# Where the adjacency's checks are computed: row sums and zero-or-one test in the convolutions' passes, casting transfers in the attention stage

## The chip, the core and the metric

The kernel runs on one core of one Trainium2 chip. The time is the device time of one execution in microseconds (us). A core has a matrix engine (TensorE, PE in the profile, with its weight loads as PEld), a vector engine (VectorE, DVE), an engine for activations (ScalarE, ACT), a general one (GpSimd, POOL) and SyncE (SP), which here only issues transfers. Each takes its instructions in a fixed order; they meet at semaphores. Transfers (DMA) are issued by SP, ACT or POOL and moved by 16 DMA engines.

## What is computed

Sixteen graphs (batches) of N = 1024 nodes with D = 128 features each and a symmetric zero-or-one adjacency go through four residual layers, each after a layer norm and a relu:

```python
h = relu(layernorm(x)); x = x + three_convolutions(h, dilate(adj))   # layer 0
h = relu(layernorm(x)); x = x + attention(h, adj)                    # 4 heads, log(adj) added to the scores
h = relu(layernorm(x)); x = x + graph_attention(h, adj)              # 4 heads, softmax over neighbours
h = relu(layernorm(x)); x = x + normalised_sum(h, adj)               # layer 3
...
A_hat = adj + eye; deg = sum(A_hat, axis=2); d_inv = deg ** -0.5     # used in layer 3
```

Layer 0 removes neighbours row by row, then convolves three times: `agg = adj_d @ h / deg`, `out = agg @ Wr + h @ Wx + b`, rows normalised, relu, and a batch norm over all nodes of all graphs, which forces one pass over all sixteen graphs per convolution.

## The kernel before

The program has three stages after a short one for the weights. `P` = 128 rows make a block, so a graph has `NB` = 8 blocks; `HN` = 512 is half a row.

`dilate_plain` (to about 690 us) holds all sixteen adjacencies in fp8, loaded by casting transfers that POOL issues (L727, L729: 32-bit in memory, fp8 in the core), and writes the thinned ones to memory as `kept`, with the reciprocal degrees `rdeg`.

`convolutions_plain` (about 690 to 1604 us) makes a first pass over the graphs (layer norm, transposes, the neighbours' sum), two middle passes (convolution l = 0 and 1 with the sum for the next one) and a last one. A scheduler orders its instructions. In `neighbours`, one graph's thinned adjacency `C` (1 MB) and its reciprocal degrees spread over the partitions, `rdb` (512 KB), come in by SP; `h` is transposed into `hT`, split into three bf16 parts on ACT and DVE (L676 to L679), and 48 matmuls (`g`, L1040) make the sum, which DVE scales into `aggT` (L1042). A convolution reads `aggT` and `hT` (`o`, L1093 and L1094), squares on ACT (`sq`, L1099), sums on DVE (L1100), takes a power on POOL (L1045) and applies it on ACT (`h`, L1106). `hT` goes to memory as `spill`.

`attentions_plain` (about 1604 us to the end) runs layers 1 to 3 of several graphs side by side. Seven generators (`matrices`, `before`, `attend`, `values`, `positive`, `gat`, `gcn`) each yield an engine, an expected duration, the time that they need and a change in the number of PSUM banks; the planner `in_order` picks the step that can start first and so writes out one order for all engines. `before` loads `x` and the three `spill`ed results (`h_a`, `hT_a`, by SP) and finishes layer 0. `attend` puts the adjacency into PSUM (L1408, ACT), adds the scores (L1413, PE) and takes the exponential (L1421, ACT). `positive` and `gat` are layer 2, `gcn` is layer 3.

`matrices` brings in the untouched adjacency of each graph in fp8, as `A` (four buffers), and computes what the program must know of it. For each of the eight row blocks it loads 512 KB in 32 bits (L1309, two buffers), and ACT turns it into fp8 and sums the rows at the same time into `deg` (L1310). DVE tests that each value is zero or one, with the count of others in `trouble` (L1314). PE subtracts the transposed blocks (L1321, L1323) and ACT sums the absolute difference (L1327), which tests the symmetry. At the end `verdict` looks at `trouble`, and a slow general version, which is not needed for these inputs, runs if anything was found.

Of the kernel before, what the change touches and what calls it, by code (L numbers as in the profile page):

```python
# [6 lines left out]
F32 = mybir.dt.float32  # L7
# [11 lines left out]
P = 128  # L19
# [942 lines left out]
def convolutions_plain(tc, x, ident, ap, xp, h0, minus_half, kept, rdeg, spill, final, Wr, Wx, bias, gamma, beta, Wl, bl):  # L962
    nc = tc.nc
    with ExitStack() as ctx:
# [3 lines left out]
        w2 = ctx.enter_context(tc.tile_pool(name="c_work", bufs=2))  # L968
        pso = ctx.enter_context(tc.tile_pool(name="c_out", bufs=4, space=PSUM))
# [50 lines left out]
        def neighbours(b, h):  # L1020

            C = ap.tile([P, NB, N], F8, name="C")
            nc.sync.dma_start(C, kept[b])
            rdb = w2.tile([P, N], F32, name="rdb")
            nc.sync.dma_start(rdb, rdeg[b][None, :].to_broadcast([P, N]))
            for hf in range(2):
                ps = pst.tile([P, HN], F32, name="t")
                for c in range(4):
                    nc.tensor.transpose(ps[:, c * P:(c + 1) * P], h[:, 4 * hf + c, :], ident)  # L1029
                nc.scalar.copy(hT[b][:, hf * HN:(hf + 1) * HN], ps)  # L1030
            parts = w2.tile([P, 3, NB, D], BF16, name="parts")
            for m in range(2):
                half = slice(4 * m, 4 * m + 4)
                Splitter(nc)(h[:, half], [parts[:, k, half] for k in range(3)])
            for hf in range(2):
                cols = slice(hf * HN, (hf + 1) * HN)
                ps = psg.tile([P, HN], F32, name="g")
                for j in range(NB):
                    for k in range(3):
                        nc.tensor.matmul(ps, parts[:, k, j, :], C[:, j, cols],  # L1040
                                         start=j == 0 and k == 0, stop=j == NB - 1 and k == 2)
                nc.vector.tensor_tensor(aggT[b][:, cols], ps, rdb[:, cols], op=ALU.mult)  # L1042

        def rsqrt(out, v):
            nc.gpsimd.tensor_tensor(out, v, minus_half[:, :v.shape[-1]], op=ALU.pow)  # L1045

        for b in range(B):
# [15 lines left out]
            neighbours(b, h)  # L1063
            if b == 1:
                wr = [matrix(w, f"wr{i}") for i, w in enumerate(Wr)]
                wx = [matrix(w, f"wx{i}") for i, w in enumerate(Wx)]
                wl = final[:3]
                for i, t in enumerate(wl):
                    nc.sync.dma_start(t, Wl[i * D:(i + 1) * D])
                gam = [column(v, f"gam{i}") for i, v in enumerate(gamma)]  # L1070
                bet = [column(v, f"bet{i}") for i, v in enumerate(beta)]
                b6 = [row6(v, f"b6_{i}") for i, v in enumerate(bias)]
                last = row6(bl, "bl6")

        wr_s, wx_s, constant = wr[0], wx[0], row_parts(b6[0], "const0")
        for l in range(3):
            stats = kp.tile([P, 2 * B, 6], F32, name="stats")
            for b in range(B):
                if l:
                    rd6 = xp.tile([6, N], F32, name="xt")  # L1080
                    nc.sync.dma_start(rd6, rdeg[b][None, :].to_broadcast([6, N]))
                    has = w2.tile([6, N], BF16, name="has")
                    nc.vector.tensor_scalar(has, rd6, floor, None, op0=ALU.is_gt)
# [19 lines left out]
                rsqrt(nrm[:, 1, :], nrm[:, 0, :])  # L1103
                h = w2.tile([P, NB, D], F32, name="h")
# [3 lines left out]
                if l < 2:  # L1108
                    neighbours(b, h)
                else:  # L1110
                    for hf in range(2):
# [23 lines left out]
            if l < 2:  # L1135
# [4 lines left out]
                row = small.tile([6, D], F32, name="row")  # L1140
# [8 lines left out]
        nc.vector.tensor_copy(final[3][0:3], row_parts(last, "const3")[0:3])  # L1149

# [55 lines left out]
def attentions_plain(tc, x, spill, final, ready_weights, adj, deg, trouble, eye, out, scores, bound, reach):  # L1206
    nc = tc.nc
    with ExitStack() as ctx:
# [7 lines left out]
        lp = ctx.enter_context(tc.tile_pool(name="f_load", bufs=2))  # L1216
# [28 lines left out]
        nc.vector.memset(trouble, 0.0)  # L1245
# [54 lines left out]
        def matrices():  # L1300

            for b in range(B):
# [3 lines left out]
                for i in range(NB):  # L1306
                    t = yield "ACT", 1.3, 0.0, 0
                    a = lp.tile([P, N], F32, name="a")
                    nc.sync.dma_start(a, adj[b, i * P:(i + 1) * P, :])  # L1309
                    nc.scalar.activation(m[:, i, :], a, AF.Relu, accum_out=deg[:, b, i:i + 1], saturate=False)  # L1310
                    yield "DVE", 1.4, 0.0, 0
                    junk = lp.tile([P, N], F8, name="junk", bufs=1)

                    nc.vector.scalar_tensor_tensor(junk, a, 0.0, a, op0=ALU.is_gt, op1=ALU.not_equal,  # L1314
                                                   accum_out=trouble[:, b, i, 0:1], saturate=False)
                    for hf in range(2):
                        w = min(HN, (i - 4 * hf) * P)
                        if w > 0:
# [8 lines left out]
                            nc.scalar.activation(junk[:, :w], ps[:, :w], AF.Abs, accum_out=trouble[:, b, i, 1 + hf:2 + hf])  # L1327
# [412 lines left out]
def whole(tc, x, adj, nodemask, chunk_mats, chunk_mask, eye, sel, p, out):  # L1740
    nc = tc.nc
    with tc.tile_pool(name="dram", bufs=1, space=DRAM) as dp, tc.tile_pool(name="keep", bufs=1) as kp:
# [7 lines left out]
        trouble = kp.tile([P, B, NB, 3], F32, name="trouble")  # L1750
# [11 lines left out]
        with tc.tile_pool(name="final", bufs=1) as fp:  # L1762
            final = [fp.tile([P, D], F32, name=f"final{i}") for i in range(3)] + [fp.tile([3, D], BF16, name="final_row")]
            with tc.tile_pool(name="early", bufs=1) as yp, tc.tile_pool(name="c_adj", bufs=2) as ap, \
                    tc.tile_pool(name="c_x", bufs=2) as xp:
                ident = yp.tile([P, P], F32, name="ident")
                nc.sync.dma_start(ident, eye)
                minus_half = yp.tile([P, NB], F32, name="minus_half")
# [4 lines left out]
                convolutions_plain(tc, x, ident, ap, xp, h0, minus_half, kept, rdeg, spill, final, *layer0)  # L1773
# [46 lines left out]
```

## Time and profile before

| What | us |
|---|---|
| Runs before (three) | 4033.46, 4037.02, 4050.93; median 4037.02 |
| The profiled execution | 4039.04, span 4037.3 |
| PE busy | 3474.4 (86%) |
| DVE busy | 2527.9 (63%) |
| ACT busy | 2401.7 (59%) |
| POOL busy | 794.7 (20%) |
| Mean granted TensorE clock | 0.926 |

The page divides the span into 40 slices of 101 us; each digit is the busy share of a slice in tenths. The rows for PE, DVE, ACT and DMA show the three stages: dilation in the first seven slices, convolutions in the next nine, attention after that.

```profile
PE   4888887999999987778989988998898989989775
DVE  4988774543344343328776876776777686777656
ACT  3778764543333334676667776767666767766540
DMA  9632223443333312411221221122122022111000
```

A line of a group names the source line, the engine, the operation, the tile written and those read, the shape and the number of instructions; then busy time, mean nanoseconds of one, the engine's idle time before them and what ended most of it. [...]

### The profile page before, as it was taken

Reading aid. Unit: us, or ns where it says so; the run is one execution under the profiler, and the core shown is the slowest. Engines: PE = TensorE matmul, PEld = TensorE weight load, DVE = VectorE, ACT = ScalarE, POOL = GpSimd, SP = SyncE. Lnnn points to the kernel's source line nnn. Section 1 sums busy time; section 2 is a strip of 40 time slices with the busy share of each in tenths; the row PEclk is TensorE's granted clock in tenths of the full one; section 3 lists DMA queues with packets and bytes.
Section 4 is the critical chain, followed back from the end, with each engine's and each line's share of the span. In section 5 each row is a group of like instructions: output and inputs, shape, how many; then the busy total and the mean of one; then the engine's idle time right before and its main releaser. Section 6 shows DMA issues by size and latency. Waiting matters only on the chain.

```text
span 4037.3 us, 65855 instructions
## 1 busy us (share of the span) xinstructions
PE 3474.4 (86%) x26756; PEld 1998.6 (50%) x26756; DVE 2527.9 (63%) x4782; ACT 2401.7 (59%) x3961; POOL 794.7 (20%) x680
## 2 busy tenths in 40 slices
PE   4888887999999987778989988998898989989775
PEld 2556565445555566324444444444454444454333
DVE  4988774543344343328776876776777686777656
ACT  3778764543333334676667776767666767766540
POOL 7545521210000011101111112112111101211110
PEclk9999887999999998799999998999998999999887
DMA  9632223443333312411221221122122022111000
GB/s 106 40 21 16 14 97 116 165 159 126 125 111 121 108 68 85 142 37 53 74 79 43 64 79 60 51 74 74 43 69 80 26 74 79 58 59 48 27 17 17
DMA packets 182500, 293.21 MB, mean 73 GB/s; under 512 B 77468, under 2 KB 124456, under 8 KB 173992
## 3 DMA queue, kind: packets, MB, share of 16 engines
q1 hardware_dynamic: 91944, 221.69, 16.8%
q0 software_dynamic: 79728, 24.66, 7.5%
q10 hardware_dynamic: 10512, 42.54, 2.6%
q8 instruction: 212, 3.47, 0.4%
q14 instruction: 104, 0.85, 0.1%
HBM read 287.98 MB, written 51.19 MB: 84 GB/s over the span
## 4 chain that ended last, share of the span: by engine, by line
PE 58%; DVE 15%; ACT 7%; DMA 3%; issue 2%; POOL 2%; ACTq 0%; SPq 0%; POOLq 0%; DVEq 0%
PE g L1040 12%; PE acc L1444 9%; PE sum L1570 9%; PE t L1413 5%; PE sum L1624 4%; PE sum L1555 4%; DVE pm L1495 3%; PE o L1093 2%; PE sum L1357 2%; PE o L1094 2%; PE sum L1375 1%; ACT e L1421 1%; DVE rden L1450 1%; PE t L1029 1%; PE sum L1295 1%
## 5 line engine op out<-in xcount | busy, mean ns | idle before, releaser
L1421 ACT ACTIVATE e<-t 128x1024 f32<-128x1024 f32 x512 | 508.2, 1023 | 489.3 <-PE t L1413 472.9
L1495 DVE SCALAR_TENSOR_TENSOR pm<-dst,minus,A 128x1024 fp8e4<-128x1024 f32 x512 | 676.2, 1350 | 7.9 <-DMA dst<-scores 7.9
L1040 PE MATMUL g<-C,parts 128*128 128x512 fp8e4 x2304 | 521.3, 381 | 15.4 <-DVE aggT L1042 9.2
L1408 ACT ACTIVATE t<-A 128x2048 f32<-128x2048 fp8e4 x256 | 482.3, 1884 | 3.9 <-ACT dst L1475 0.3
L1570 PEld LDWEIGHTS <-pm 128*128 128x128 fp8e4 x4096 | 347.0, 98 | 187.1 <-issue 165.3
L1570 PE MATMUL sum<-parts,pm 128*128 128x198 bf16 x4096 | 400.3, 251 | 26.0 <-DVE pm L1495 16.3
L1444 PE MATMUL acc<-e,va 128*32 128x512 f32 x2048 | 330.5, 616 | 41.3 <-ACT e L1421 38.4
L1040 PEld LDWEIGHTS <-parts 128*128 128x128 bf16 x2304 | 223.1, 98 | 262.7 <-ACT parts L678 5.7
L1413 PE MATMUL t<-qT,kT 32*128 32x512 f32 x2048 | 307.7, 672 | 31.7 <-ACT t L1408 31.3
L1444 PE MATMUL acc<-e,ones_hd 128*32 128x512 f32 x2048 | 319.7, 601 | 0.0
L1573 DVE TENSOR_REDUCE pos<-sum 128x132 f32<-128x396 f32 x256 | 145.0, 566 | 204.0 <-PE sum L1570 203.4
L1555 PE MATMUL sum<-parts,A 128*128 128x396 bf16 x1024 | 210.8, 351 | 44.2 <-DVE parts L1547 23.9
L1042 DVE TENSOR_TENSOR aggT<-g,rdb 128x512 f32<-128x512 f32 x96 | 66.2, 690 | 269.2 <-PE g L1040 269.1
L1045 POOL TENSOR_TENSOR nrm<-nrm,minus_half 128x8 f32<-128x8 f32 x48 | 79.6, 1662 | 639.8 <-DVE nrm L1102 639.8
L1624 PE MATMUL sum<-A,gparts 128*128 128x512 fp8e4 x768 | 178.0, 385 | 24.9 <-ACT gparts L1607 17.6
L835 DVE TENSOR_TENSOR r<-ya,both 128x512 bf16<-128x512 f16 x184 | 140.2, 776 | 92.7 <-ACT ya L832 91.9
L1099 ACT ACTIVATE sq<-o 128x512 f32<-128x512 f32 x96 | 55.8, 599 | 226.1 <-PE o L1094 224.3
L1267 POOL TENSOR_TENSOR ln_st<-ln_st,minus_half 128x8 f32<-128x8 f32 x48 | 86.1, 1794 | 511.8 <-DVE ln_st L1265 377.1
L882 DVE SCALAR_TENSOR_TENSOR rows<-y,thirty,rows 128x1024 fp8e4<-128x1024 f16 x128 | 169.9, 1335 | 25.4 <-ACT y L874 24.6
L1555 PEld LDWEIGHTS <-A 128*128 128x128 fp8e4 x1024 | 94.5, 99 | 182.0 <-issue 104.1
L1106 ACT ACTIVATE h<-o,nrm 128x128 f32<-128x128 f32 x384 | 105.7, 384 | 116.9 <-POOL nrm L1045 113.7
L885 POOL TENSOR_TENSOR own<-rows,lower 128x256 bf16<-128x256 fp8e4 x128 | 109.5, 866 | 330.6 <-DVE rows L882 197.2
(287 smaller groups left out, 6937.7 us busy)
## 6 DMA issues: line engine op xcount, KB each, us to landing
a<-in_adj_dram SPq DMA_DIRECT2D x128, 512.0 KB
C<-kept SPq DMA_DIRECT2D x48, 1024.0 KB
dst<-scores SPq DMA_DIRECT2D x64, 512.0 KB
rdb<-rdeg SPq DMA_DIRECT2D x48, 512.0 KB
spill<-hT ACTq DMA_DIRECT2D x48, 512.0 KB
kept<-rows ACTq DMA_DIRECT2D x16, 1024.0 KB
h_a<-spill SPq DMA_DIRECT2D x64, 256.0 KB
hT_a<-spill SPq DMA_DIRECT2D x16, 512.0 KB
```

The source lines that it names most:

```text
L835: nc.vector.tensor_tensor(r, ya, both[:, 1, :, None].to_broadcast([P, G, P]), op=ALU.is_equal)
L882: nc.vector.scalar_tensor_tensor(row, y16, hh[:, g:g + 1], row, op0=ALU.not_equal, op1=ALU.mult, saturate=False)
L1040: nc.tensor.matmul(ps, parts[:, k, j, :], C[:, j, cols], start=j == 0 and k == 0, stop=j == NB - 1 and k == 2)
L1408: nc.scalar.activation(s, A[b][:, k, None, cols].to_broadcast([P, H, HN]), AF.Copy, scale=16.0)
L1413: nc.tensor.matmul(s[:, hd], kT[r, k * P:(k + 1) * P], qT[r, cols], start=False, stop=True, skip_group_check=True)
L1421: nc.scalar.activation(es[:, hd:hd + 2], s[:, hd:hd + 2], AF.Exp, scale=SIGMA)
L1444: nc.tensor.matmul(ps[r], ones if one else va[:, k, r], es[:, hd], start=k == 0, stop=k == NB - 1)
L1495: nc.vector.scalar_tensor_tensor(pm[:, i, :], dst[hd], minus[:, i, hd:hd + 1], A[b][:, i, :], op0=ALU.is_ge, op1=ALU.mult, saturate=False)
L1555: nc.tensor.matmul(ps[:, :3 * H * W], A[b][:, i, j * P:(j + 1) * P], parts4[:, i, :, :, W:], start=i == 0, stop=i == NB - 1)
L1570: nc.tensor.matmul(ps[:, jj * 6 * W:(jj + 1) * 6 * W], pm[:, i, (j + jj) * P:(j + jj + 1) * P], flat(parts4[:, i, hd]), start=i == 0, stop ...
L1573: nc.vector.reduce_sum(pos[:, j:j + 2, hd, :], ps[:, :12 * W].rearrange("p (j s w) -> p j w s", j=2, s=3), axis=AX.X)
L1624: nc.tensor.matmul(ps, parts[:, k, m, :], A[b][:, m, cols], start=m == 0 and k == 0, stop=False)
```

## The change

The row sums and the zero-or-one test leave the attention stage. A new function `look(n)` in the convolutions does n half row blocks (128 x 512): it loads one (256 KB, SP, three buffers), sums its rows on ACT with a relu whose result is thrown away, and tests it on DVE. It is called at several points of each pass, 256 times in all, and the two half sums are added into `deg` at the end of the stage. In the attention stage `matrices` loads each row block straight into fp8 by a casting transfer that POOL issues; the symmetry test stays. For room in the core's memory `rdb`, `has`, `row` and the attention's load pool get one buffer instead of two or three. `trouble` gets four columns, and its clearing moves to the start of the program, to POOL.

```diff
+        lp = ctx.enter_context(tc.tile_pool(name="c_load", bufs=3))
...
-            rdb = w2.tile([P, N], F32, name="rdb")
+            rdb = w2.tile([P, N], F32, name="rdb", bufs=1)
...
                 nc.scalar.copy(hT[b][:, hf * HN:(hf + 1) * HN], ps)
+            look(1)
             parts = w2.tile([P, 3, NB, D], BF16, name="parts")
...
+        halves = cp.tile([P, B, NB, 2], F32, name="halves")
+        parts_of = [(b, i, hf) for b in range(B) for i in range(NB) for hf in range(2)]
+
+        def look(n):
+
+            for b, i, hf in [parts_of.pop(0) for _ in range(n)]:
+                cols = slice(hf * HN, (hf + 1) * HN)
+                a = lp.tile([P, HN], F32, name="a")
+                nc.sync.dma_start(a, adj[b, i * P:(i + 1) * P, cols])
+                m = lp.tile([P, HN], F8, name="m", bufs=1)
+                nc.scalar.activation(m, a, AF.Relu, accum_out=halves[:, b, i, hf:hf + 1], saturate=False)
+                junk = lp.tile([P, HN], F8, name="junk", bufs=1)
+                nc.vector.scalar_tensor_tensor(junk, a, 0.0, a, op0=ALU.is_gt, op1=ALU.not_equal,
+                                               accum_out=trouble[:, b, i, 2 + hf:3 + hf], saturate=False)
...
             neighbours(b, h)
+            look(3)
...
-                    has = w2.tile([6, N], BF16, name="has")
+                    has = w2.tile([6, N], BF16, name="has", bufs=1)
...
                 rsqrt(nrm[:, 1, :], nrm[:, 0, :])
+
+                look(2 if l < 2 else 1)
...
                 if l < 2:
                     neighbours(b, h)
+                    look(2)
                 else:
+                    look(1)
...
-                row = small.tile([6, D], F32, name="row")
+                row = small.tile([6, D], F32, name="row", bufs=1)
...
+        nc.vector.tensor_tensor(deg, halves[:, :, :, 0], halves[:, :, :, 1], op=ALU.add)
...
-        lp = ctx.enter_context(tc.tile_pool(name="f_load", bufs=2))
+        lp = ctx.enter_context(tc.tile_pool(name="f_load", bufs=1))
...
-        nc.vector.memset(trouble, 0.0)
...
                 for i in range(NB):
-                    t = yield "ACT", 1.3, 0.0, 0
-                    a = lp.tile([P, N], F32, name="a")
-                    nc.sync.dma_start(a, adj[b, i * P:(i + 1) * P, :])
-                    nc.scalar.activation(m[:, i, :], a, AF.Relu, accum_out=deg[:, b, i:i + 1], saturate=False)
-                    yield "DVE", 1.4, 0.0, 0
-                    junk = lp.tile([P, N], F8, name="junk", bufs=1)
-
-                    nc.vector.scalar_tensor_tensor(junk, a, 0.0, a, op0=ALU.is_gt, op1=ALU.not_equal,
-                                                   accum_out=trouble[:, b, i, 0:1], saturate=False)
+                    t = yield "POOL", 0.9, 0.0, 0
+                    nc.gpsimd.dma_start(m[:, i, :], adj[b, i * P:(i + 1) * P, :])
+                    t += 8.0
...
+                nc.gpsimd.memset(trouble, 0.0)
```

## The prediction

> **What bounds the kernel now.** I read the table of busy time by stretch first. The dilation ends at about 690 us, the convolutions at about 1604 us, the attention stage at the end. Columns: stretch, length, then busy microseconds of PE, PEld, DVE, ACT and POOL with counts, granted clock, DMA share, GB/s.
>
> ```profile
> 690.00:747.00 57.00, 44.22 (x198) 22.30 (x197) 32.21 (x140) 27.87 (x61) 14.54 (x11) 0.83 0.51 167
> 747.00:923.00 176.00, 174.57 (x891) 90.03 (x889) 83.99 (x232) 83.88 (x191) 26.64 (x20) 1.00 0.45 159
> 923.00:1460.00 537.00, 513.49 (x2831) 311.22 (x2830) 213.38 (x384) 193.59 (x478) 50.23 (x32) 0.97 0.32 116
> 1460.00:1604.00 144.00, 119.83 (x800) 97.37 (x799) 54.96 (x103) 69.91 (x192) 27.21 (x16) 0.87 0.15 58
> 1604.00:1850.00 246.00, 184.92 (x1114) 81.62 (x1118) 96.74 (x187) 171.69 (x250) 26.73 (x15) 0.87 0.30 95
> 1850.00:3500.00 1650.00, 1478.46 (x11155) 790.38 (x11148) 1182.39 (x1749) 1136.14 (x1548) 270.23 (x142) 0.95 0.20 63
> 3500.00:3750.00 250.00, 218.94 (x1691) 117.47 (x1689) 189.04 (x251) 155.87 (x203) 30.90 (x15) 0.97 0.17 52
> 3750.00:4037.00 287.00, 200.64 (x1364) 110.81 (x1364) 170.83 (x246) 101.74 (x128) 38.52 (x22) 0.82 0.07 21
> ```
>
> TensorE is the bound nearly everywhere: 99% busy in the first pass (747 to 923), 96% in the two middle passes, 90% in the steady attention stage. The change takes nothing from PE. So it can gain only where PE idles in the attention stage (61 + 172 + 31 + 86 = 350 us) and lose where it makes PE idle in the convolutions, where ACT and DVE are only 36 to 48% busy.
>
> Next the groups that move, and PE's waits from 1850 to 3500 us (engine and line, what it waited for, total us, times, longest).
>
> ```profile
> L1314 DVE SCALAR_TENSOR_TENSOR junk<-a 128x1024 fp8e4<-128x1024 f32 x128 | 157.9, 1233 | 23.8 <-DMA a<-in_adj_dram 23.5
> L1310 ACT ACTIVATE A<-a 128x1024 fp8e4<-128x1024 f32 x128 | 135.3, 1058 | 31.4 <-DMA a<-in_adj_dram 31.4
> ```
> ```profile
> PE sum L1295 <- DVE oT L1452: 27.8, 5, 9.1
> PE t L1413 <- ACT t L1408: 27.1, 16, 4.0
> PE sum L1357 <- DMA h_a<-spill: 22.6, 9, 6.1
> PE sum L1321 <- ACT A L1310: 13.6, 4, 6.2
> PE sum L1555 <- DVE tot L1558: 13.3, 11, 3.0
> PE sum L1555 <- DVE parts L1547: 12.1, 4, 4.5
> ```
>
> PE's idle time is many short waits with different releasers; only L1310 and part of h_a belong to the work that leaves.
>
> Last, the SP queue's own waits and two pairs of pieces from the chain, which give the passes' rhythm.
>
> ```profile
> SPq L1309 <- DVE junk L1314: 885.9, 116, 65.8
> ```
> ```profile
> 747.04 20.33 PE g L1040 x92
> 771.02 19.86 PE g L1040 x92
> ...
> 923.34 9.50 PE g L1040 x44
> ...
> 974.25 9.50 PE g L1040 x44
> ```
>
> The first says that the adjacency loads, with two buffers, hold SP's queue until DVE has read them, and the loads behind them (h_a, hT_a) with it. The others: two batches take 24 us in the first pass, three take 50.9 us in the middle ones.
>
> [...]
>
> **Part by part, attention stage.**
> Removed: on ACT 128 × (1.058 + 0.196 accumulator read, source view of L1310) = 160 us, on DVE 128 × (1.233 + 0.083) = 168 us, on SP 128 issues of 0.33 us and the queue's blocking. Added on POOL: 128 casting issues; L727, the same form, takes 0.59 us each, 76 us on an engine that is 16% busy. They stand in front of the `pow` steps on POOL, at most one or two issues at a time (the order of the built program shows mostly one to three), so 1 us on a few chains, taken as nothing. Landing: 9.8 us in the crowded start of the dilation, 4.4 to 4.9 for 64 to 80 KB later. The planner allows 8 us before PE's symmetry check; from 0 to about 30 us of PE waiting, I take 0. PE's checks L1321 to L1323 and ACT's L1327 stay.
>
> What PE gains:
> - Start (1604 to 1850): PE idles 61 us and ACT is 70% busy. The chain here has 5.4% on adjacency loads, 3.2% on L1310 and 4.7% on h_a loads, of 246 us: 13 + 8 + 12. The first two go, half of the third (its other half is that buffer's own release): 27, less 2 for the casting loads that start with the stage: 25 us. Bounds 10 to 40.
> - Steady stretch: A 13.6, half of h_a 11; waits ended by ACT or DVE otherwise sum to about 135 us in the same view. ACT falls from 69 to 62%, DVE from 72 to 65%. As an estimate a queueing wait goes with u/(1-u), so 27% of what is queueing; I take a third of 135 as that, the rest as plain latency: 12. Sum 36 us. Bounds 5 (latency is the whole of it) to 90.
> - From 3500 on: the chain is latency of the last batches; 0, from -10 to +15.
> Together 61 us.
>
> **Convolutions.** Added: 256 pieces (128x512 each). On ACT 0.60 (L1099, the same width) + 0.20 - 0.1 overlap, so 0.70 to 0.80, 0.75 taken: 192 us. On DVE 0.68 (L1100) + 0.08: 195 us. On SP 256 issues of 0.33 = 84 us and 67 MB. The scheduler pulls the pieces forward: in the built program ACT has 81 before the first spill, 125 during the first of the two middle passes, 50 in the second, none later. Per three batches that is 25 pieces.
> - Room in a middle pass: 50.9 us less 36% that ACT is busy = 32.5, over 25: 1.30 us a piece. In the first pass, nine per pair: (24 - 11.4)/9 = 1.40.
> - Need: with three buffers a buffer's round is issue 0.33 + landing 2.95 + operation 0.75 + hops 0.25 = 4.3, so 1.43 us a piece once the three loaded ahead are used, 0.75 before. ACT takes them in groups of 8, 2, 2, 6, 1, 1, 5: 15 are loaded ahead, 10 paced, mean 1.02. It fits, so PE's matmuls should hide most of it.
> - What isn't hidden: DVE and ACT steps on the path from o to g (sq, norm, pow, h, transposes, parts) come up to a piece later each; g already starts within 1 us of its parts. I take 0.5 us per batch over 27 batches with pieces = 14 us, bounds 0 and 40. At the start, batch 1's normalisation stands behind five pieces and the second rdb load behind eight: 5 × 1.43 = 7 us, plus 3.
> - rdb, has and row with one buffer: the next rdb load waits for the product of the batch before, but it is needed only about 10 us later, at the first half's end; nothing. C is issued about 11 us before use; six pieces in front cost 3 × 0.33 + 3 × 1.43 = 5 us and its landing about 5: just covered, and if not, the loss is part of the rival below.
> - The memset of trouble on POOL goes ahead of the dilation's first loads: 1 us.
> Together 25 us. DMA share in a middle pass: 116 + 25 × 0.262 MB / 50.9 us = 245 GB/s; 116 is a share of 0.32, so about 0.68.
>
> **Sum.** The profiled execution took 4039.0 us (span 4037.3). 4039 - 61 + 25 = 4003; it lies 2 us above the median of the runs shown, so 4001.
>
> **Rivals.**
> 1. Slower: the pieces pace the passes. In SP's one queue, C and rdb wait for a batch's end, and pieces behind them wait along; pieces that load beside a 1 MB C land in 4.7 us (the longest such wait on a 256 or 512 KB load in the chain) and not 2.95. Then a round is 6.0, 2.0 us a piece, none loaded ahead. Against the room of 1.30 and 1.40 that is 175 × 0.7 + 81 × 0.6 = 171 us at worst; I put it at a mean of 1.8: 175 × 0.5 + 81 × 0.4 = 120, less 61: 4096. It decides from a mean of about 1.57 us on, where the loss reaches the gain. For it: three buffers, engines in order, PE at 96 to 99% with nothing to spare. Against it: groups are short, ACT has half its time free.
> 2. Nothing: the attention stage's waits are latency, gain 30, loss 25: 4032.
> 3. More: the lighter ACT and DVE let the planner pack PE; all 36 becomes 90 and the start gives 40: 3930.
> That the casting loads come late (30 us of PE waits) would turn the main case into the second.
>
> **Numbers.** Forecast 0.47 (own range 3955 to 4017), rival 3 0.10, rival 2 0.15, rival 1 0.28. About 0.5%, 20 us, is what a measurement tells from no change: faster 0.57, same 0.15, slower 0.28. Range 3920 to 4095: the steady stretch's upper bound below; above, rival 1 up to its central price.
>
> **What will show it.** Right: L1310 and the full-row L1314 gone; attention from its first to last instruction about 60 us shorter with ACT near 62% in the middle; first exponential earlier; first and middle passes with PE still over 93% busy and rhythms under 25 and 53 us. Wrong: PE waiting for C or parts in the passes, ACT's pieces waiting for adjacency loads by more than 50 us in sum with `sq` or `h` behind them; or PE's L1321 waiting for the casting loads.

## The result, and the profile after

The changed kernel takes 4025.81 us (median of 20 runs), the kernel before 4041.07 us in the runs beside it: ratio 0.9969, interval 0.9959 to 0.9978. By the ratio that is a gain of 0.3%, about 13 us (the medians are 15 us apart), where 36 us were forecast. The profiled executions are only 3 us apart, with spans of 4037.3 us before and 4034.2 us now, and the parts below are read from these two.

The small difference hides two large ones. The batch norm's `scale` on POOL ends each convolution, so the last of its three starts marks the border between the convolutions and the attention stage. The view of that tile gives number, durations in nanoseconds, and first and last start, first for the kernel before, then for the changed one:

```profile
L1045 POOL TENSOR_TENSOR scale<-mv,minus_half x3: 552/552/552, 1153.3 to 1605.9; 128x1 f32<-128x1 f32 x3
```
```profile
L1047 POOL TENSOR_TENSOR scale<-mv,minus_half x3: 552/553/553, 1242.4 to 1714.4; 128x1 f32<-128x1 f32 x3
```

The convolutions are 109 us longer (25 forecast), and the attention stage is 2319.8 us instead of 2431.4, 112 us shorter (61 forecast). Of the 109 us, 89 are there before the first `scale`.

Busy time by stretch in the changed kernel; the borders are the three `scale` steps and two points in the attention stage (columns as in the prediction's first table):

```profile
690.00:950.00 260.00, 225.64 (x1062) 114.48 (x1059) 166.11 (x542) 165.37 (x413) 39.20 (x30) 0.92 0.69 230
950.00:1242.40 292.40, 245.02 (x1264) 148.25 (x1264) 172.59 (x401) 176.24 (x475) 26.11 (x15) 0.92 0.64 211
1242.40:1552.70 310.30, 282.35 (x1566) 171.38 (x1564) 149.56 (x312) 137.24 (x354) 27.13 (x18) 0.94 0.43 150
1552.70:1714.40 161.70, 136.02 (x850) 105.34 (x850) 62.06 (x121) 69.88 (x192) 27.73 (x18) 0.84 0.14 55
1714.40:1962.00 247.60, 202.60 (x1313) 93.50 (x1316) 81.99 (x153) 160.40 (x215) 37.82 (x39) 0.91 0.28 54
1962.00:3602.00 1640.00, 1514.77 (x11562) 806.24 (x11555) 1122.02 (x1607) 1076.88 (x1407) 318.34 (x239) 0.97 0.21 44
3602.00:4034.20 432.20, 340.45 (x2451) 190.14 (x2449) 282.44 (x413) 194.20 (x252) 69.39 (x43) 0.89 0.10 24
```

PE is 87 and 84% busy in the first two stretches, where the kernel before has 94% up to 923 us and 97% from there to its first `scale` (these lines stand in the last section), while ACT and DVE are no more than 59 to 64% busy. Not one engine is full: they wait for each other. What ACT and DVE wait for stands in the groups of the page (busy us, mean ns, idle before and its cause):

```profile
L1063 DVE SCALAR_TENSOR_TENSOR junk<-a 128x512 fp8e4<-128x512 f32 x256 | 176.0, 688 | 146.2 <-DMA a<-in_adj_dram 142.7
L1061 ACT ACTIVATE m<-a 128x512 fp8e4<-128x512 f32 x256 | 161.9, 632 | 171.7 <-DMA a<-in_adj_dram 168.6
```

Each piece costs about as much waiting as working. From the chain of waits of the stretch 890 to 950 us (start, length, what):

```profile
895.16 7.07 DMA a<-in_adj_dram
...
905.54 8.15 DMA a<-in_adj_dram
...
914.56 3.41 DMA a<-in_adj_dram
...
919.69 6.73 DMA rdb<-rdeg
...
932.41 8.32 DMA a<-in_adj_dram
...
941.58 2.53 DMA a<-in_adj_dram
```

SP issued `C` and `rdb` just ahead of the three long ones (`rdb` at 894.75, 905.12 and 931.99): a piece of 256 KB that is issued right behind them takes 7 to 8 us, and `rdb` itself 6.7. Two pieces that are issued 9 to 10 us after `rdb` take 3.4 and 2.5 us. What this does to PE is in PE's waits from 690 us to the first `scale`, of the kernel before and of the changed one (total us, times, longest):

```profile
PE g L1040 <- DVE aggT L1042: 9.2, 3, 4.1
PE t L1029 <- ACT h L1106: 7.5, 5, 1.5
```
```profile
PE g L1042 <- DVE aggT L1044: 33.8, 16, 4.6
PE t L1030 <- ACT h L1128: 25.3, 5, 7.1
PE g L1042 <- ACT parts L678: 10.9, 8, 3.1
PE g L1042 <- DVE parts L679: 7.1, 3, 4.1
```

PE hardly waits for a piece itself. It waits for the convolution's own steps, and those stand behind a piece in ACT's or DVE's queue, which waits for its load. Three middle graphs take 61 to 62 us instead of 50.9 (the powers on POOL start at 1011.68, 1072.61, 1134.81 and 1196.37): 25 pieces in 61.5 us are 2.46 us a piece, a round of 7.4 us for each of three buffers. SP waited 253 times for a reader to free a buffer (169 times for DVE, 84 for ACT, 417 us in all), about as often as there are loads, so the buffers do pace them.

One such stretch in the timeline of the changed kernel, of ACT and then of DVE (start, us; in brackets the wait and its cause):

```profile
1123.33 0.63 ACT L1061 ACTIVATE m<-a 128x512 fp8e4<-128x512 f32 x1 [7.00 <-DMA a<-in_adj_dram]
```
```profile
1123.34 0.69 DVE L1063 SCALAR_TENSOR_TENSOR junk<-a 128x512 fp8e4<-128x512 f32 x1 [4.77 <-DMA a<-in_adj_dram]
...
1126.78 0.69 DVE L1063 SCALAR_TENSOR_TENSOR junk<-a 128x512 fp8e4<-128x512 f32 x1 [0.80 <-DMA a<-in_adj_dram]
1127.93 0.69 DVE L1063 SCALAR_TENSOR_TENSOR junk<-a 128x512 fp8e4<-128x512 f32 x1 [0.45 <-DMA a<-in_adj_dram]
1129.11 0.69 DVE L1063 SCALAR_TENSOR_TENSOR junk<-a 128x512 fp8e4<-128x512 f32 x1 [0.48 <-DMA a<-in_adj_dram]
```

Both engines stand still together until 1123.3, after SP issued the next `C` at 1110.9 and `rdb` at 1112.6, and ACT a `spill` of 512 KB at 1114.2. Some microseconds later, with only pieces in flight, these follow each other at 1.15 us, which is faster than the forecast's 1.43. So a load is not slow by itself.

PE is not idle during that wait: its `g` runs from 1115.5 to 1125.2. The delay reaches it one step later. The chain goes on over three loads of pieces to a graph's power, which stands behind them:

```profile
1118.03 6.30 DMA a<-in_adj_dram
...
1126.06 2.96 DMA a<-in_adj_dram
...
1129.88 3.88 DMA a<-in_adj_dram
...
1134.81 1.65 POOL nrm L1047
```

The power lets ACT make `h`, and PE's next transposes (`t`), at 1136.9, have waited 7.1 us for it, the longest wait in the list above.

In the attention stage PE idled 61 us at the start and 172 in the middle before. Four of the five largest waits named in the prediction shrink, and that for `tot` doesn't: from 1962 to 3602 us (the same length as before's 1850 to 3500, less ten) PE now waits

```profile
PE t L1432 <- ACT t L1427: 17.7, 13, 4.0
PE sum L1320 <- DVE oT L1471: 15.2, 4, 9.0
PE sum L1574 <- DVE tot L1577: 13.1, 11, 2.9
...
PE sum L1376 <- DMA h_a<-spill: 7.3, 3, 3.1
...
PE sum L1340 <- DMA A<-in_adj_dram: 4.6, 2, 2.9
```

against 27.1 (t), 27.8 (oT), 13.3 (tot), 22.6 (h_a) and 13.6 (A).

### The profile page after: what moved, and what is told of

Same layout as the page of the kernel before. It is cut to its first block, busy times and chain, and to the rows that moved or that the text cites. A ratio compares the mean times of both kernels' runs of the same rounds, so it can differ in the third digit from the quotient of the medians.

```text
span 4034.2 us, 67273 instructions
## 1 busy us (share of the span) xinstructions
PE 3489.3 (86%) x26756; PEld 2007.6 (50%) x26756; DVE 2542.3 (63%) x5038; ACT 2441.3 (61%) x4217; POOL 854.0 (21%) x809
## 4 chain that ended last, share of the span: by engine, by line
PE 46%; DVE 17%; ACT 8%; DMA 7%; issue 5%; POOL 3%; ACTq 0%; SPq 0%; POOLq 0%; DVEq 0%
PE acc L1463 9%; PE sum L1589 8%; DMA a<-in_adj_dram 5%; PE t L1432 4%; DVE pm L1514 4%; PE sum L1643 4%; PE g L1042 4%; PE sum L1574 3%; POOL nrm L1047 2%; PE o L1113 2%; PE sum L1320 1%; DVE rden L1469 1%; PE sum L1394 1%; PE o L1114 1%; DVE junk L1063 1%
## 5 line engine op out<-in xcount | busy, mean ns | idle before, releaser
L1042 PE MATMUL g<-C,parts 128*128 128x512 fp8e4 x2304 | 540.8, 389 | 58.9 <-DVE aggT L1044 37.6
L1463 PE MATMUL acc<-e,va 128*32 128x512 f32 x2048 | 326.8, 621 | 25.1 <-ACT e L1440 22.5
L1432 PE MATMUL t<-qT,kT 32*128 32x512 f32 x2048 | 296.0, 648 | 19.9 <-ACT t L1427 19.8
L1063 DVE SCALAR_TENSOR_TENSOR junk<-a 128x512 fp8e4<-128x512 f32 x256 | 176.0, 688 | 146.2 <-DMA a<-in_adj_dram 142.7
L1061 ACT ACTIVATE m<-a 128x512 fp8e4<-128x512 f32 x256 | 161.9, 632 | 171.7 <-DMA a<-in_adj_dram 168.6
L882 DVE SCALAR_TENSOR_TENSOR rows<-y,thirty,rows 128x1024 fp8e4<-128x1024 f16 x128 | 168.1, 1321 | 26.1 <-ACT y L874 25.3
L1113 PE MATMUL o<-wr,aggT 128*128 128x128 f32 x768 | 177.8, 318 | 0.0
L872 PE MATMUL big<-tri,rows 128*128 128x256 fp8e4 (+3 forms) x896 | 175.2, 317 | 0.3 <-ACT H L877 0.2
```

The costliest lines, as they stand in the source:

```text
L872: nc.tensor.matmul(ps[:, k * P:], lhs, triF[:, :HN - k * P], start=k == 0, stop=k == 3)
L1042: nc.tensor.matmul(ps, parts[:, k, j, :], C[:, j, cols], start=j == 0 and k == 0, stop=j == NB - 1 and k == 2)
L1113: nc.tensor.matmul(o, aggT[b][:, rows], wr_s, start=False, stop=False)
L1432: nc.tensor.matmul(s[:, hd], kT[r, k * P:(k + 1) * P], qT[r, cols], start=False, stop=True, skip_group_check=True)
L1463: nc.tensor.matmul(ps[r], ones if one else va[:, k, r], es[:, hd], start=k == 0, stop=k == NB - 1)
```

## The experiments

Two questions: what makes the convolutions 109 us longer, and what makes the attention stage 112 us shorter. For the first, theory 1 was the buffers (three of them, each held until the later of ACT and DVE has read it: 7.4 us a round), theory 2 the added transfers beside `C` and `rdb`, theory 3 the pieces' own time on ACT and DVE. For the second, theory A was the relief of SP's queue, theory B that of ACT and DVE.

All results first. Marks are the first and third start of `scale` in the profiled execution, in us; the ratio is to the kernel before in the runs beside each.

| Kernel | First scale | Third scale | From there to the end of the span | Median of runs | Ratio (interval) |
|---|---|---|---|---|---|
| before | 1153.3 | 1605.9 | 2431.4 | 4041.1 | 1 |
| changed | 1242.4 | 1714.4 | 2319.8 | 4025.8 | 0.9969 (0.9959 to 0.9978) |
| nopieces | 1151.0 | 1600.9 | 2314.8 | 3917.1 | 0.9708 (0.9683 to 0.9734) |
| noload | 1185.6 | 1642.9 | 2311.1 | 3959.1 | 0.9808 (0.9778 to 0.9838) |
| loadonly | 1216.1 | 1669.1 | 2313.8 | 3982.0 | 0.9862 (0.9842 to 0.9881) |
| loadquarter | 1157.7 | 1610.6 | 2317.1 | 3924.6 | 0.9717 (0.9687 to 0.9748) |
| sumonly | 1213.3 | 1676.8 | 2313.1 | 3994.1 | 0.9893 (0.9877 to 0.9910) |
| buf4 | 1250.2 | 1707.0 | 2314.8 | 4021.3 | 0.9961 (0.9949 to 0.9972) |
| ring4 | 1193.5 | 1640.2 | 2318.6 | 3959.1 | 0.9807 (0.9790 to 0.9823) |
| ring5 | 1180.6 | 1633.0 | 2309.6 | 3940.2 | 0.9762 (0.9737 to 0.9786) |
| ring5late | 1162.7 | 1657.6 | 2325.1 | 3986.0 | 0.9873 (0.9856 to 0.9889) |
| ring6 | 1173.9 | 1626.5 | 2309.6 | 3944.8 | 0.9782 (0.9761 to 0.9803) |
| ring6even | 1165.4 | 1633.1 | 2309.2 | 3950.7 | 0.9792 (0.9774 to 0.9811) |
| castkeep | 1156.8 | 1607.1 | 2403.5 | 4015.6 | 0.9952 (0.9934 to 0.9969) |
| notest | 1149.5 | 1603.7 | 2364.3 | 3971.5 | 0.9842 (0.9824 to 0.9860) |

In every variant of the changed kernel the attention stage takes 2309 to 2325 us, whatever the convolutions do, so the third `scale` carries nearly the whole difference between them.

### The pieces taken apart

**nopieces**

> The changed kernel without any of the 256 pieces: no row sums (deg is set to 30) and no zero-or-one test; the attention stage is as changed. It separates the pieces from the rest of the change. If the loss in the convolutions (third scale at 1714.4 us instead of 1605.9) is the pieces' in any way (buffers, transfers or engine time), the third scale comes back to 1600 to 1612 us and the whole time is about 4026 - 109 = 3917 us. If the single buffers for rdb, has and row cost something of their own, the scale stays above 1615 us, and the last pass, which has no pieces and yet is 6.8 us longer after the change, stays at 161 us. The attention stage should need the changed kernel's 2320 us in both cases.

```diff
-                a = lp.tile([P, HN], F32, name="a")
-                nc.sync.dma_start(a, adj[b, i * P:(i + 1) * P, cols])
-                m = lp.tile([P, HN], F8, name="m", bufs=1)
...
+                pass
...
-        nc.vector.tensor_tensor(deg, halves[:, :, :, 0], halves[:, :, :, 1], op=ALU.add)
+        nc.vector.memset(deg, 30.0)
```

The third `scale` is at 1600.9 us, even 5 us before that of the kernel before. The loss belongs to the pieces alone; the single buffers of `rdb`, `has` and `row` cost nothing in sum. The last pass is 155.2 us, as before. The bases for what follows are 1151.0 and 1600.9: against them the changed kernel's loss is 113 us.

**noload**

> All 256 pieces stay on ACT and DVE, but each reads one block that is loaded once, so no piece waits for a transfer or a buffer (the sums and the test are of that one block). Theory 1 (round of a buffer) and theory 2 (crowded transfers): the loss falls from 109 us to what the operations themselves cost, about the 25 us that were forecast, at most 45: third scale at 1630 to 1650 us. Theory 3 (the operations' own time in ACT's and DVE's queues is the loss): third scale stays above 1685 us.

```diff
+        fixed = lp.tile([P, HN], F32, name="a", bufs=1)
+        nc.sync.dma_start(fixed, adj[0, 0:P, 0:HN])
...
-                a = lp.tile([P, HN], F32, name="a")
-                nc.sync.dma_start(a, adj[b, i * P:(i + 1) * P, cols])
+                a = fixed
```

Third `scale` at 1642.9 us: the operations alone, in the order that they get here, cost 42 us. The windows show where: with no buffer to hold them, the scheduler puts more pieces into the first pass.

```profile
690.00:950.00 260.00, 223.84 (x1061) 115.37 (x1060) 217.96 (x709) 216.18 (x550) 45.49 (x31) 0.93 0.40 135
950.00:1185.60 235.60, 224.63 (x1233) 132.96 (x1232) 145.67 (x318) 162.09 (x429) 24.27 (x15) 0.99 0.35 125
```

DVE and ACT are 84 and 83% busy in the first row and PE 86%; in the second PE is at 95% again. Theory 3 alone (over 1685 us) is out.

**loadonly**

> The changed kernel with the 256 loads alone: nothing reads the pieces (row sums and test are left out, deg is 30). If the added 67 MB crowd out the loads of C and rdb that the passes need (theory 2), the loss stays above 40 us and PE waits for C. If not, the third scale is at 1600 to 1612 us as without pieces, and the traffic by itself costs nothing.

```diff
-                m = lp.tile([P, HN], F8, name="m", bufs=1)
-                nc.scalar.activation(m, a, AF.Relu, accum_out=halves[:, b, i, hf:hf + 1], saturate=False)
...
```

Third `scale` at 1669.1: loads that nobody reads cost 68 us. PE doesn't wait for `C`, as was expected; DVE's waits from 690 to 1216 us say how the loss comes about:

```profile
DVE aggT L1044 <- DMA rdb<-rdeg: 125.6, 16, 13.7
```

`aggT` is the step that PE's `g` waits for, and it stands up to 13.7 us for `rdb`. The same view of the kernel without pieces has 10.7 us of this in two waits, that of the kernel before none. 68 and 42 make 110 of the 113 us, but this isn't shown to be a division of the loss: up to its first `scale` the changed kernel waits only 11.9 us for `rdb`, and 131.5 and 111.7 us in ACT's and DVE's pieces, where loadonly has no pieces to wait. Where readers hold the buffers back, the same bytes cost time at another place.

**loadquarter**

> The kernel with the loads alone (row sums and test left out, deg is 30), and of each piece only the first quarter: 256 loads as before, of 64 KB instead of 256 KB, at the same places of SP's queue. The loads alone cost 68 us up to the third scale (1669 against 1601 us without pieces). Theory 2 (what the added bytes take from C and rdb on the DMA engines): the loss falls to a quarter or less, third scale at 1600 to 1618 us. Theory 1b (a fixed time per load, in SP's queue in front of C and rdb): the loss stays over 45 us, third scale above 1645 us.

```diff
-                nc.sync.dma_start(a, adj[b, i * P:(i + 1) * P, cols])
+                nc.sync.dma_start(a[:, :P], adj[b, i * P:(i + 1) * P, hf * HN:hf * HN + P])
```

The third `scale` comes at 1610.6: 10 us of loss instead of 68. The first two stretches of loadonly and of loadquarter:

```profile
690.00:950.00 260.00, 223.55 (x1043) 111.65 (x1042) 109.50 (x362) 107.84 (x241) 41.54 (x31) 0.91 0.83 277
950.00:1150.00 200.00, 176.11 (x918) 108.84 (x916) 66.80 (x116) 68.76 (x167) 16.36 (x10) 0.90 0.75 256
```
```profile
690.00:950.00 260.00, 244.26 (x1201) 125.67 (x1201) 121.89 (x383) 120.91 (x275) 44.69 (x33) 0.96 0.62 203
950.00:1150.00 200.00, 193.91 (x1073) 119.23 (x1072) 77.85 (x132) 77.86 (x192) 19.64 (x12) 0.97 0.42 144
```

As many loads in the same places of SP's queue, but a quarter of the bytes: the DMA share falls from 0.83 to 0.62 in the first stretch and the wait for `rdb` from 125.6 to 38.1 us. Of these loads the bytes cost, not the issues; another issuing engine for the pieces wasn't tried.

**sumonly**

> The changed kernel without the zero-or-one test (DVE's half of each of the 256 pieces is left out); loads, three buffers and ACT's row sums stay, in nearly the same places (24 pieces to three middle batches). Theory 1a (a buffer is held until the later of ACT and DVE has read it, and the other engine then stands at its next piece): with one reader the skew is gone; a buffer's round falls from 7.4 to about 4.5 us, three middle batches take 51 to 55 us, the loss up to the third scale falls from 109 to 30 to 50 us. Theory 1b (the loads stand in SP's queue behind C and rdb and beside them on the DMA engines, whoever reads them): three batches stay at 58 to 61 us, loss 85 us or more. Theory 3 (engine time): half the operations, loss about 60 us, in equal parts per piece.

```diff
-                junk = lp.tile([P, HN], F8, name="junk", bufs=1)
-                nc.vector.scalar_tensor_tensor(junk, a, 0.0, a, op0=ALU.is_gt, op1=ALU.not_equal,
-                                               accum_out=trouble[:, b, i, 2 + hf:3 + hf], saturate=False)
```

Third `scale` at 1676.8, a loss of 71 us over the kernel before: outside all three numbers, nearest to theory 3. Three graphs take 55 to 58 us. Next to loadonly (63 us over before), ACT's row sums add only 8 us, DVE's test after that 38. How much of the 38 is the test's own time and how much the buffer held for a second reader isn't told apart.

### Buffers or order

**buf4**

> Four load buffers instead of three (two small tiles with one buffer less make room). The built program then has 31 pieces to three batches and is through with them at the 17th batch of the middle passes. Theory 1: a round of 7.4 us over four buffers is 1.85 us a piece, so 31 pieces need 57 us: three batches in 57 to 59 us, and this for 16 batches instead of some 21; the loss up to the third scale falls to about 60 to 75 us. Theory 2 (what the transfers bring is shared): 2.46 us a piece stay, three batches take about 76 us, and the loss stays near 109 us. Theory 3: 31 pieces instead of 25 in three batches: the loss per batch grows by a quarter, the sum stays near 109 us.

```diff
-        lp = ctx.enter_context(tc.tile_pool(name="c_load", bufs=3))
+        lp = ctx.enter_context(tc.tile_pool(name="c_load", bufs=4))
```

Three graphs take 60 us with 31 pieces, 1.94 us each, near theory 1's 1.85. But the loss up to the third `scale` is 101 us, not 60 to 75, though ACT's pieces wait only 106.3 us for their loads instead of 168.6. A buffer more lets the scheduler pull more pieces forward: 246 instead of 207 stand before the first `scale`, and the DMA engines move 238 GB/s from 690 to 950 us and 237 from there to 1150 us instead of 230 and 211. Theory 1 has the rate nearly right, but the number of buffers isn't what sets the loss.

**ring5**

> The pieces take their buffers from the ring of sq (five in all instead of two and three, the same memory), so that they stay with their batch: in the built program 15 pieces stand to three middle batches instead of 25, and 4 to a batch of the last pass instead of none. Theory 1: a buffer's round of about 7.4 us over three buffers is 2.46 us a piece; 15 pieces then need 37 us of the 50.9 us that three batches take, and are hidden: the rhythm of three middle batches is 52 to 55 us instead of 61, the third scale at 1635 to 1665 us. Theory 2: fewer transfers beside a batch, the same direction, but loads still take 5 us and more. Theory 3: as many operations as before, only elsewhere: the loss stays near 109 us, third scale above 1690. If sq has to wait for a piece's buffer the loss is larger than 109 us.

```diff
-                a = lp.tile([P, HN], F32, name="a")
+                a = w2.tile([P, 4, D], F32, name="sq", bufs=5).rearrange("p c d -> p (c d)")
...
-                    sq = w2.tile([P, 4, D], F32, name="sq")
+                    sq = w2.tile([P, 4, D], F32, name="sq", bufs=5)
```

The same pieces, the same number of tiles in all, but in a ring with `sq`, where a piece can't run far ahead of its graph. Third `scale` at 1633.0, 27 us over the kernel before, and 3940 us in all: 96 us faster than the kernel before (4036.0 beside it) and 2% faster than the changed one. That is a little better than theory 1 allowed (1635 to 1665), and three middle graphs take 50 to 52 us. Its passes (the last three borders are its own `scale` steps):

```profile
690.00:950.00 260.00, 231.07 (x1143) 119.63 (x1140) 158.87 (x523) 163.03 (x400) 44.51 (x32) 0.93 0.65 224
950.00:1180.60 230.60, 218.74 (x1196) 131.65 (x1195) 136.07 (x293) 131.53 (x362) 22.28 (x14) 0.98 0.59 201
1180.60:1474.50 293.90, 278.22 (x1576) 168.43 (x1575) 171.20 (x375) 151.65 (x416) 27.32 (x18) 0.97 0.54 187
1474.50:1633.00 158.50, 130.81 (x840) 103.68 (x837) 82.05 (x184) 88.31 (x256) 29.98 (x18) 0.87 0.31 109
```

The second middle pass carries 80 pieces in 293.9 us, where the kernel before takes 297.7 without any. The last pass carries 32, two to a graph and not four as expected. Over the whole kernel ACT's pieces wait 22.5 us for their loads instead of 168.6, and DVE's 54.2 instead of 142.7, for the same bytes. Of the 27 us, 23 are lost by the fourth graph of the first middle pass (its power starts at 961.53 instead of 938.12); before that the pieces still stand thickest. The ring and the order come together here: no run holds the pieces in place in buffers of their own.

**ring4**

> As the ring of five, with four tiles for sq and pieces together, so less buffering than the changed kernel has (two and three), but the pieces spread alike (15 to three middle batches, two to a batch in the last pass). If the place of the pieces decides (order), the time stays within 15 us of the ring of five, 3940 to 3955 us. If the number of buffers decides, sq waits for pieces: the loss is back, over 3990 us.

As ring5 with `bufs=4`. Fewer tiles than the changed kernel has, and 3959 us: 66 us faster than it, though 4 us over the expected 3940 to 3955. The place of the pieces decides most; a fifth tile is worth another 19 us.

**ring6 and ring6even**

> The ring with six tiles (two small tiles with one buffer less make room). Four gave 3959 us, five 3940. If the remaining loss up to the third scale (27 us over before) is the ring's own scarcity, a sixth takes half of it again: 3930 us. If it is the loads beside C, rdb and x at the start, or engine time, nothing more comes: 3938 to 3943 us.

> The ring of six with one piece less per batch at the start and one more in the second middle pass (three, five, six and two to a batch). The first pass should give back about a quarter of its 23 us, 6 us; the second middle pass, which with five pieces to a batch lost nothing, should still have room for six (18 to three batches of 50.9 us): 3925 to 3935 us. If that pass is at its limit, it is longer by 5 to 20 us: 3940 to 3955 us.

```diff
-            look(3)
+            look(2)
...
-                look(2 if l < 2 else 1)
+                look((2, 3, 1)[l])
```

ring6 has `bufs=6`; ring6even adds these lines. Ratios of 0.9782 and 0.9792 overlap with that of ring5, 0.9762. A sixth tile brings nothing that shows, so the ring's size isn't what costs ring5 its remaining 27 us. In ring6even the first `scale` is 8.5 us earlier than in ring6 and the third 6.6 us later: the second middle pass takes 308.3 us instead of 293.8, so six pieces to a graph are too many for it.

**ring5late**

> The ring of five with the pieces moved later: two instead of four to a batch at the start, four instead of two in the last pass (37 instead of 69 before the first spill). The ring of five still loses some 23 us up to the third batch of the first middle pass. If that is the pieces' crowd at the start, it halves: third scale 1618 to 1625 us, about 3928 us in all. If the last pass (PE 83% busy there) has no room for four pieces a batch, it is longer than 155 us and the gain is given back: 3940 us.

```diff
-            look(3)
+            look(1)
...
-                look(2 if l < 2 else 1)
+                look(2)
...
-                    look(1)
+                    look(2)
```

The first `scale` is at 1162.7, 12 us over nopieces instead of 30 for ring5: most of what ring5 still loses there comes from the crowd at the start. But the last pass takes 203.8 us instead of 158.5, and 3986 us is the result, worse than either expectation. In its last pass two graphs take 24 us where they took 17, ACT and DVE are only 52 and 51% busy, and POOL's power waits for the sums of `sq` 168 us in all (117 in ring5). Since `sq` shares its ring with the pieces, this may be the ring's order and not a lack of room; no run separates the two.

### The attention stage

**castkeep**

> The kernel before with one part of the change: the fp8 matrices come by casting transfers on POOL's queue, and ACT's row sums and DVE's test stay in the attention stage (of the cast values, with fp8 operands). The convolutions are as before, third scale at 1606 us. Which part gives the attention stage its 112 us (2431 before, 2320 after)? Theory A (the adjacency loads no longer hold SP's queue, and no operation of ACT and DVE waits for them): most of it stays, 80 us or more, about 3950 us in all. Theory B (ACT and DVE have less to do, which lets PE's work follow closer): at most 35 us stay, 4005 us or more.

```diff
+                    t = yield "POOL", 0.9, 0.0, 0
+                    nc.gpsimd.dma_start(m[:, i, :], adj[b, i * P:(i + 1) * P, :])
+                    t += 8.0
+                    yield "ACT", 1.3, t, 0
+                    junk = lp.tile([P, N], F8, name="a", bufs=1)
+                    nc.scalar.activation(junk, m[:, i, :], AF.Relu, accum_out=deg[:, b, i:i + 1], saturate=False)
...
```

**notest**

> The kernel before without the zero-or-one test on DVE in the attention stage (left out: the test of every entry): DVE has 168 us less, ACT's cast with row sums and the loads on SP's queue stay, a load buffer is free once ACT has read it. Theory B: the relief of one of the two engines brings about half, 40 to 65 us: 3975 to 3998 us. Theory A: SP's queue still waits for ACT, 25 us or less: 4014 us or more.

```diff
-                    yield "DVE", 1.4, 0.0, 0
-                    junk = lp.tile([P, N], F8, name="junk", bufs=1)
-
-                    nc.vector.scalar_tensor_tensor(junk, a, 0.0, a, op0=ALU.is_gt, op1=ALU.not_equal,
-                                                   accum_out=trouble[:, b, i, 0:1], saturate=False)
```

castkeep's attention stage is 2403.5 us, 28 less than before; notest's is 2364.3, 67 less, just over the 40 to 65 that were expected by theory B. Of the change's 112 us the casting transfers alone bring a quarter, so theory A alone is out. Leaving out DVE's test brings over half, but that isn't theory B alone: with one reader less the load buffers come free sooner, SP's queue waits 730.4 us for them instead of 885.9, and over twelve graphs PE's waits for `h_a` and `A` fall from 17.2 and 13.6 us to 5.6 and 5.8. How much of the 67 us is DVE's shorter queue and how much the earlier loads isn't separated, and ACT's relief was not tried alone. Each of these kernels also has its own order from the planner. PE's waits over the twelve graphs between the first and the thirteenth result, in castkeep:

```profile
PE t L1415 <- ACT t L1410: 40.4, 25, 4.0
PE sum L1557 <- DVE tot L1560: 29.3, 17, 4.2
...
PE sum L1359 <- DMA h_a<-spill: 8.2, 4, 2.5
```

With the loads off SP's queue the wait for `h_a` falls from 17.2 to 8.2 us, and instead of 13.6 us for `A` on ACT's cast PE waits 6.3 us for the transfer. But the waits for ACT's `t` and DVE's `tot` grow from 26.1 and 16.3 us to 40.4 and 29.3: with as much to do on both engines as before, they take the place of much of what went, and PE's idle time falls only from 175.2 to 154.3 us.

## Why the prediction came out as it did

The direction was right and the size was not: 4001 forecast, 4026 measured. Both terms of its sum were too small, the loss by 84 us and the gain by 51.

**The step that failed: the pieces' need against their room.** The prediction had "so 1.43 us a piece once the three loaded ahead are used, 0.75 before", and "mean 1.02. It fits, so PE's matmuls should hide most of it." Measured: 2.46 us a piece in the middle pass and a rhythm of 61.5 us, not under 53. The forecast had worked out the traffic itself (245 GB/s, share 0.68; measured 211 to 230, 0.64 to 0.69) and made nothing of it: it priced every landing at 2.95 us, which no run shows as the price of a piece in the passes. That is near the shortest `h_a` load of 256 KB in the chain of the kernel before, 2.93 us in an attention stage with a DMA share of 0.19 (the others in the chain take 3.0 to 4.7); the pieces in the chains above take 2.5 to 8.3. The 0.25 for hops was the author's estimate. Pieces with nothing beside them do better than that (1.15 us apart, a round of 3.45 us for three buffers instead of 4.3); pieces right behind `C` and `rdb` take 7.1 to 8.3 us. The forecast's round had no term for the loads that stand in front; the measured one is 7.4 us in the middle pass.

Rival 1 had named the place, the pieces beside `C` and `rdb`, with landings of 4.7 us (not the longest in the chain, where a row block of 512 KB takes 6.06 us at 1621.8). Its loss of 120 us, near the 109 measured, is luck: its sum with the measured 2.46 gives 175 × 1.16 + 81 × 1.06 = 289 us. What a piece needs beyond its room isn't simply added to a pass, as PE can work on during a wait, like `g` in the timeline above: the rhythm grew by 10.6 us for 25 pieces, not by 29.

**A term at nothing: PE's own time.** "The change takes nothing from PE" holds for the number of matmuls, not for their time. PE is busy 37 us longer in the convolutions and 25 us less in the attention stage (the last section has the lines), and the forecast had neither. So the loss of 109 us is 72 us of idle time and 37 of slower matmuls.

**Within that loss, the start.** 10 us were forecast up to the second graph's normalisation; the first pass and the first three graphs of the next lost 44 (the fourth graph's power starts at 981.71 instead of 938.12), half of it by the last layer norm (its power starts at 876.73 instead of 854.81). 81 pieces ran before the first `spill` at 933.3 us, 57 of them before that last power. The rest of the first middle pass lost another 45 us, the second 13 and the last pass 7.

**The steps behind a piece** were 14 us, with 40 as upper bound; noload has 42 for all that the operations cost, in its own order.

**Attention, start:** 25 forecast, 27 measured (first finished graph 341.2 us after the third `scale` instead of 368.3). castkeep and notest get 18 and 23 of it, each alone, and 7 of the 27 are PE's shorter busy time, so the sum is right in part by luck.

**Attention, steady stretch:** A and half of h_a were 24.6 us; measured 9.0 and 15.3, together 24.3. The term that failed is the next one, a third of ACT's and DVE's 135 us as queueing, "the rest as plain latency: 12"; that such waits go with u/(1-u) was the author's estimate, and no run shows it. From the first to the thirteenth graph 65 us were gained (1688.1 to 1623.3). PE's idle time fell by 48 of them (175.2 to 126.9), so about 24 us came on top of `A` and `h_a`, twice the 12. The other 17 are again PE's busy time (1512.9 to 1496.3 us, clock 0.97 instead of 0.95). ACT and DVE were relieved by less than forecast, to 66 and 68% of the middle stretch and not to 62 and 65. And the nothing from 3500 us on was 20 (375.0 to 355.3 us for the last three graphs), nearly all of it idle time of PE. Rival 3's 90 for the stretch was too much; its reason, lighter ACT and DVE, fits notest, but whether the planner's order or the shorter queues do it isn't shown.

**What held:** the casting loads (4.9 us to landing; PE waits 4.6 us for them), the single buffers, 0.75 us a piece on ACT (632 ns and 187 ns for the accumulator read; the two overlap by about 0.1 us, and pieces follow at 0.75 to 0.76 us), and the sign that was to show the forecast wrong: ACT's pieces wait for adjacency loads by 131.5 us up to the first `scale`, over the 50 given. The last pass is 6.8 us longer with no piece in it; PE is busy 136.0 us there instead of 127.8, at a granted clock of 0.84 instead of 0.87. By the clocks' ratio, as an estimate, that is 4.6 us; the rest stays open.

## What to carry to other kernels

Background work that would fit into an engine's idle share on average can still stop it: price its bytes beside the loads that the main work needs in that stretch, and look at where the scheduler puts it. A buffer more let it crowd to the front here. Taking its tiles from the ring of a tile that each main step uses ties it to that step, at no memory; here this turned a gain of 13 us into one of 96. And where many short waits for two busy engines keep the bound engine idle, less work on those engines can give back more than their named waits suggest: here, over twelve graphs, 48 us of idle time where 24 were named, and 17 us of shorter matmuls.

## What the runs showed of the hardware

In the stretches with more stalls, PE's own work is slower too. The convolutions of the kernel before, and its attention stage as a whole:

```profile
690.00:923.00 233.00, 218.79 (x1087) 112.32 (x1086) 116.20 (x371) 111.75 (x251) 41.18 (x31) 0.96 0.46 161
923.00:1153.30 230.30, 222.92 (x1219) 134.04 (x1218) 90.83 (x155) 89.64 (x222) 22.92 (x15) 0.98 0.35 125
1153.30:1451.00 297.70, 282.63 (x1576) 173.61 (x1575) 119.36 (x215) 103.95 (x256) 26.77 (x18) 0.95 0.31 112
1451.00:1605.90 154.90, 127.76 (x840) 100.94 (x837) 59.94 (x118) 69.91 (x192) 27.75 (x17) 0.87 0.14 57
1605.90:4037.00 2431.10, 2082.96 (x15318) 1100.29 (x15318) 1637.20 (x2427) 1565.45 (x2128) 366.38 (x193) 0.93 0.19 60
```

Between 690 us and the third `scale` PE is busy 852 us in the kernel before and 889 in the changed one, for the same work, at a mean granted clock of 0.95 and 0.91 over the whole of it. As an estimate, 852 × 0.95 / 0.91 = 890, so the ratio of the clocks would account for the 37 us. A `g` matmul is busy for 237 ns on average up to 950 us and for 236 from there to the first `scale`, against 226 in both stretches of the kernel before. In the attention stage it goes the other way: 2083 us busy before and 2058 after (15318 matmuls each), at 0.93 and 0.95. PE idles 64 us of the convolutions before and 135 of the changed ones, 348 and 262 us of the attention stage, and PE's longest wait up to the first `scale` is 4.1 us before and 7.1 in the changed kernel. That stalls and a lower clock come together is shown; whether the stalls are the reason isn't.

The mean share of the DMA engines didn't tell how long a load waits: at 0.69 in the first stretch, 256 KB loads right behind `C` and `rdb` took 7 to 8 us and others 2.5 to 3.4, and in the second, at 0.64, 1.15 us from piece to piece was to be had some microseconds after `C` and `rdb` were in.
